# Grouped query attention with a sigmoid-routed expert layer on one core: query projections without padding, spread over partition quadrants by transfers inside SBUF

## The chip, the cores and the metric

The kernel runs on one core of one Trainium2 chip, in one launch. The metric is the device time of that core in microseconds (us). Three runs of the kernel before took 600.33, 602.37 and 600.90 us, so its median is 600.90 us. All data are float32.

Engine names: PE is TensorE (matmuls; PEld its weight loads), DVE is VectorE, ACT is ScalarE, POOL is GpSimd, SP is SyncE. SBUF and PSUM have 128 partitions each; a quadrant is 32 consecutive partitions.

## The reference, cut to what matters

`x` is (2, 1024, 256). It passes an attention layer, a layer norm, an expert layer with a shared expert, and a second layer norm:

```python
def _L0_attn_ref(x, Wq, Wk, Wv, Wo):          # 16 query heads of 16, 4 key/value heads
    q = (x @ Wq).reshape(B, T, N_HEAD, HEAD_DIM).transpose(0, 2, 1, 3)
    k = (x @ Wk).reshape(B, T, N_HEAD_KV, HEAD_DIM).transpose(0, 2, 1, 3)
    v = (x @ Wv).reshape(B, T, N_HEAD_KV, HEAD_DIM).transpose(0, 2, 1, 3)
    k = jnp.repeat(k, rep, axis=1)             # rep = 4
    v = jnp.repeat(v, rep, axis=1)
    att = jnp.einsum('bhqd,bhkd->bhqk', q, k) * scale
    att = att + alibi[None] + causal[None, None]
    att = jax.nn.softmax(att, axis=-1)
    y = jnp.einsum('bhqk,bhkd->bhqd', att, v)
    return y.transpose(0, 2, 1, 3).reshape(B, T, C) @ Wo
...
x = _layernorm(x + _L0_attn_ref(x, ...), axis=-1)
x = _layernorm(x + _L0_ffn_ref(x, ...), axis=-1)   # 8 experts, one per token, and a shared one
```

`alibi` is a slope of the head times (key position minus query position); the four query heads that share a key head have the same slope. `causal` is minus infinity above the diagonal. Only the attention layer's query projection, `x @ Wq`, and what stands around it in time are touched by the change.

## The kernel before, in words

**Tiles.** There are 16 tiles of 128 tokens, 8 for each of the two sequences `b`. A *half* `(b, i)` is four tiles, 512 tokens; there are four halves: (0,0), (0,4), (1,0), (1,4). `KC` = 2 is the number of 128-row pieces of the 256 input channels; every projection sums over both pieces `c` in PSUM.

**Layout for the scores.** A key head `g` (0 to 3) has the quadrant of partitions 32g to 32g+31. In it, partition 0 (`ROW_POS`) carries the position term, partition 1 (`ROW_MAX`) takes the negated row maximum later, and partitions 16 to 31 (`ROW_HEAD`) the 16 channels of the head. `kT` holds keys so (`wk_pad` is `Wk` with zero columns in between), and `kaug` adds the positions. `qT[b]` is 128 partitions x 4 (`r`, the query heads of a key head) x 1024 tokens. Its rows come from `wq_pad` (L128 to L137), which is `Wq` spread to 128 columns for each `r`, half of them zero. A score tile is then four matmuls side by side, one in each quadrant.

**Projections of a half.** `turn_x` (L308) transposes four token tiles on PE and copies `xT` out on ACT (L317). `do_kv` (L319) makes keys (`kpj`, two matmuls of 128x512 that DVE adds `kaug` to, L323) and values (`vpj`, eight matmuls of 128x64, copied by ACT, L334). `do_q(b, r, i)` (L336) makes two of the four `r`, each with two matmuls of 128x512 (`project`, L292 to L296), and ACT adds `qbias`, the slopes in the `ROW_POS` rows, while it copies to `qT` (L341). So a half has 8 such matmuls and 4 such activations.

**Order of the work.** PE, DVE, ACT and POOL follow an order written out by hand inside `manual_schedule` (`MANUAL`, L29); SP's is left to the scheduler in the first part and set by hand in the second. `first_projections` (L357) transposes the first half (L368, copied by ACT for c = 0 and DVE for c = 1, L369), then runs `do_kv`, both `do_q` and `turn_x` of the next half. Then `LEAD` = 10 *score units* run ahead (L843 to L853): a unit is four PSUM banks of scores (`start_s`, L388, `s_ps`), two for each pair of key heads. A unit on the diagonal has two banks masked by DVE (L427) and two copied by ACT (L435) and masked by POOL (L438), and each pair is reduced by DVE from a `diag` buffer later (L449). Any other unit is reduced by DVE straight from its four banks (L417). The ten units are those of the first half's four query tiles. Between them the projections of the other three halves are put in as *fill*: a list of pieces with costs (`projections`, L345), from which pieces are taken after unit k while `left * LEAD > total * (LEAD - 1 - k)`. All of this shares six PSUM banks (`bank`, L304), so a matmul waits until DVE or ACT has emptied the bank that it is to fill.

After the tenth unit the main loop (L854) pairs score units of later query tiles with the transposed scores `t_ps` (L485) of earlier ones. These need `join_maxima` (L456: DVE, L459), `spread_maxima` (L466: PE transposes `mT`, L470, and DVE adds `qS`, L474). Exponentials (L504, L521), the product with the values (L529), output, norm and routing follow, and the expert layer ends the kernel.

**Loads.** SP issues, in this order, the four loads of `x` (L98, L103), `Wo`, the router, the shared expert's weights (L110 to L112, three of 512 KB) and the filling of the table `slot_x` in DRAM with empty rows (L281, 3900 KB from one small tile). ACT issues `Wq`, `Wk`, `Wv` (L99 to L101) first. The shared expert's weights are first used after the score units have run out, `slot_x` when the first sequence is routed.

Of the kernel before, what the change touches and what calls it, by code (L numbers as in the profile page):

```python
# [9 lines left out]
F32 = mybir.dt.float32  # L10
I32 = mybir.dt.int32
AF = mybir.ActivationFunctionType
# [4 lines left out]
P = 128  # L17
N_HEAD = 16
N_KV = 4
REP = N_HEAD // N_KV  # L20
HD = 16
PAD = 32
ROW_POS = 0
ROW_MAX = 1
ROW_HEAD = 16
# [3 lines left out]
MANUAL = {  # L29
    mybir.EngineType.PE,  # L30
    mybir.EngineType.DVE,
    mybir.EngineType.Activation,
    mybir.EngineType.Pool,
}


# [8 lines left out]
def attn_moe_postln_kernel(  # L45
# [15 lines left out]
    nc = tc.nc  # L61
    B, T, C = x.shape
    E, _, F2 = gate_up.shape
    FF = F2 // 2
    KC = C // P
    FC = FF // P
    QT = T // P
    NTT = B * QT
# [6 lines left out]
    SLOTS = (E * OWN + NO) * P  # L75
    ROW = C + 4
    NUM, WT = C, C + 1
# [29 lines left out]

    sh_gu = const.tile([P, KC, F2], F32, tag="sh_gu", name="sh_gu")
    sh_d = const.tile([P, FC, C], F32, tag="sh_d", name="sh_d")
    nc.sync.dma_start(out=sh_gu[:, :, :FF], in_=sh_gate.rearrange("(c p) f -> p c f", p=P))  # L110
    nc.sync.dma_start(out=sh_gu[:, :, FF:], in_=sh_up.rearrange("(c p) f -> p c f", p=P))
    nc.sync.dma_start(out=sh_d, in_=sh_down.rearrange("(c p) n -> p c n", p=P))  # L112

# [9 lines left out]

    wq_pad = acon.tile([P, KC, REP, N_KV, PAD], F32, tag="wq_pad", name="wq_pad")  # L128
    wk_pad = acon.tile([P, KC, N_KV, PAD], F32, tag="wk_pad", name="wk_pad")
    nc.vector.memset(wk_pad, 0.0)  # L130
    nc.vector.memset(wq_pad, 0.0)
    for c in range(KC):
        nc.vector.tensor_scalar_mul(
            wq_pad[:, c, :, :, ROW_HEAD : ROW_HEAD + HD],
            wq_raw[:, c, :].rearrange("p (g r d) -> p r g d", g=N_KV, d=HD),
            scale,
        )  # L137
        nc.vector.tensor_copy(
            wk_pad[:, c, :, ROW_HEAD : ROW_HEAD + HD],
            wk_raw[:, c, :].rearrange("p (g d) -> p g d", d=HD),  # L140
        )
# [7 lines left out]
    for g, slope in enumerate(alibi_slopes()):  # L149
# [14 lines left out]
        out=causal,  # L164
        in_=causal,
# [97 lines left out]
    with (  # L263
# [11 lines left out]
    ):  # L275
        qT, kT, xT = {}, {}, {}

        empty = shp.tile([P, ROW], F32, tag="th", name="empty")
        nc.gpsimd.memset(empty, 0.0)
        nc.gpsimd.memset(empty[:, NUM : NUM + 1].bitcast(I32), NTT * P)  # L280
        nc.sync.dma_start(out=slot_xt, in_=empty.unsqueeze(1).broadcast_to([P, SLOTS // P, ROW]))  # L281


        def pj_tile(name):
            return ps_m.tile([P, 512], F32, tag="m", name=name)
# [1 line left out]
        def own_tiles(b, xTb):  # L287
            xT[b] = xTb
            kT[b] = qkp.tile([P, T], F32, tag="kT", name=f"kT_{b}")
            qT[b] = qkp.tile([P, REP, T], F32, tag="qT", name=f"qT_{b}")  # L290

        def project(dst, b, w, cols):  # L292
            for c in range(KC):
                nc.tensor.matmul(  # L294
                    dst, lhsT=w(c), rhs=xT[b][:, c, cols], start=(c == 0), stop=(c == KC - 1)
                )  # L296

        def wq_of(r):
            return lambda c: wq_pad[:, c, r].rearrange("p g d -> p (g d)")

        def wk_of(c):
            return wk_pad[:, c].rearrange("p g d -> p (g d)")
# [5 lines left out]
        def turn_x(b, i):  # L308
            if b not in xT:

                xTb = ptp.tile([P, KC, T], F32, tag="pT", name=f"xT_{b}")
                own_tiles(b, xTb)
            for c in range(KC):
                tp = bank("xtp")
                for j in range(4):
                    nc.tensor.transpose(tp[:, ts(j, P)], xs[:, b * QT + i + j, ts(c, P)], ident)
                nc.scalar.copy(xT[b][:, c, i * P : (i + 4) * P], tp)  # L317

        def do_kv(b, i):  # L319
            cols = slice(i * P, (i + 4) * P)  # L320
            pj = bank("kpj")
            project(pj, b, wk_of, cols)
            nc.vector.tensor_add(kT[b][:, cols], pj, kaug[:, cols])  # L323
            pv = bank("vpj")[:, : 4 * N_KV * HD].rearrange("p (j g d) -> p j g d", j=4, d=HD)
            for j in range(4):
                for c in range(KC):
                    nc.tensor.matmul(
                        pv[:, j].rearrange("p g d -> p (g d)"),
                        lhsT=xT[b][:, c, ts(i + j, P)],
                        rhs=wv_sb[:, c, :],  # L330
                        start=(c == 0),
                        stop=(c == KC - 1),
                    )
            nc.scalar.copy(vs[b][:, i : i + 4, :, 0:HD], pv)  # L334

        def do_q(b, r, i):  # L336
            cols = slice(i * P, (i + 4) * P)
            for j in range(2):
                pj = bank("qpj")
                project(pj, b, wq_of(r + j), cols)  # L340
                nc.scalar.activation(qT[b][:, r + j, cols], pj, AF.Identity, bias=qbias)  # L341

        halves = [(b, i) for b in range(B) for i in range(0, QT, 4)][1:]

        def projections():  # L345


            pieces = []
            for h, after in zip(halves, [*halves[1:], None]):
                pieces.append((11, lambda h=h: do_kv(*h)))  # L350
                pieces.append((14, lambda h=h: do_q(h[0], 0, h[1])))
                if after:
                    pieces.append((4, lambda h=after: turn_x(*h)))
                pieces.append((14, lambda h=h: do_q(h[0], 2, h[1])))
            return pieces

        def first_projections():  # L357

            own_tiles(0, xTp.tile([P, KC, T], F32, tag="xT", name="xT_0"))
            cols = slice(0, 512)  # L360
            warm = bank("warm")
            zeros = mnegs[0].rearrange("p r g d -> p (r g d)")
            for i in range(2):
                nc.tensor.matmul(warm, lhsT=zeros[:, :P], rhs=zeros, start=True, stop=True)
            for c, copy in enumerate((nc.scalar.copy, nc.vector.tensor_copy)):
                tp = bank("xtp0")
                for j in range(4):
                    nc.tensor.transpose(tp[:, ts(j, P)], xs[:, j, ts(c, P)], ident)  # L368
                copy(xT[0][:, c, cols], tp)  # L369
            do_kv(0, 0)  # L370
            do_q(0, 0, 0)
            do_q(0, 2, 0)
            turn_x(*halves[0])


# [419 lines left out]
        def gap(room):  # L795
            nonlocal slot
            after_burst()
            start_route(True)
            if products and products[0][0] <= slot:
                product(*products.pop(0)[1])  # L800
                room -= 4
            room -= 4 * maxima()
            pieces(room)
            slot += 1
# [39 lines left out]
        for k in range(LEAD):  # L844
            unit = s_queue.pop(0)
            sps = [[start_s(unit, h, j) for j in range(HALF)] for h in range(2)]
            run(*[m for hs in sps for _, m in hs])
            for h in range(2):
                end_s(unit, h, [sp for sp, _ in sps[h]], h == 1)
            while fill and left * LEAD > total * (LEAD - 1 - k):  # L850
                left -= fill[0][0]
                fill.pop(0)[1]()
            gap(0)  # L853
        for n, (b, qt, kt) in enumerate(steps):  # L854
            last = n + 1 == len(steps) or steps[n + 1][:2] != (b, qt)
            made = []
            if kt != qt:
                made.append((2 * n + 2, (b, qt, kt, kt == 0, False)))
            if last:
                ready = max(2 * n + 2, 2 * first[b, qt] + (7 if qt >= 3 else 4))  # L860
                made.append((ready, (b, qt, qt, qt == 0, True)))
            if s_queue:
                unit = s_queue.pop(0)
                for h in range(2):

                    t, s = [], []
                    for j in range(HALF):
                        t.append(start_t(b, qt, kt, h, j))
                        s.append(start_s(unit, 1 - h, j))
                    run(t[0][1], s[0][1], t[1][1], s[1][1])  # L870
                    end_t(b, qt, kt, h, [tp for tp, _ in t])
                    end_s(unit, 1 - h, [sp for sp, _ in s], h == 1)
                    if h == 1:
                        products += made
                    gap(6)
            else:

                t = [[start_t(b, qt, kt, h, j) for j in range(HALF)] for h in range(2)]
                run(*[m for hs in t for _, m in hs])
                for h in range(2):  # L880
                    end_t(b, qt, kt, h, [tp for tp, _ in t[h]])
                products += made
                wide_gap()
# [13 lines left out]
    with (  # L897
# [6 lines left out]
        tc.tile_pool(name="ps_d", bufs=2, space=PSUM) as ps_d,  # L904
        tc.tile_pool(name="ps_t", bufs=2, space=PSUM) as ps_t,
        tc.tile_pool(name="rt2", bufs=1) as rtp,
        tc.manual_schedule(engines=MANUAL | {mybir.EngineType.SP}),
    ):
        wgu = wgup.tile([P, E, KC, F2], F32, tag="wgu", name="wgu")
        wd = wgup.tile([P, E, FC, C], F32, tag="wd", name="wd")  # L910
# [386 lines left out]
```

## Time and profile before

| what | value |
|---|---|
| median of 3 runs | 600.90 us (600.33 to 602.37) |
| the profiled execution | 602.41 us, of which the span from first to last instruction is 600.7 us |
| mean granted PE clock | 0.988 of full |
| PE busy | 572.7 us, 95% of the span |
| DVE, ACT, POOL busy | 344.4, 267.0, 155.4 us |
| first matmul of a score unit | 19.74 us |
| end of the last fill piece's matmuls | 65.19 us |
| start of the second group of `mT` transposes | 69.39 us |

How to read it: the page gives busy time of each engine, then the span in 40 slices (15 us each; a digit is the busy share in tenths), the DMA queues, the chain of work that ended last, and groups of equal instructions with count, busy time, mean duration and what ended the idle time before them. An arrow `out<-in` names tiles. A matmul of 128x512 in float32 stands in the trace as two records. A record of a matmul is longer (some 600 ns) than the distance to the next (some 430 ns), since they are pipelined; the chain counts the distance.

### The profile page before, as it was taken

To read this page: it belongs to the slowest core of one execution; us is meant where nothing else is said; L and a number is where in the kernel's file an instruction comes from. 1 tells how busy PE (TensorE), PEld (TensorE's weight loads), DVE (VectorE), ACT (ScalarE), POOL (GpSimd) and SP (SyncE) were. 2 spreads that over 40 slices of the span, in tenths; PEclk is the share of its full clock that TensorE was granted. 3 is DMA by queue.
4 is the path that set the end of the run, shared out by engine and by line. 5 is a ranking of instruction groups with operands and counts; after the bars stand their busy time and mean duration, and the time that the engine had idled before them with its cause. 6 is when DMAs were issued, how large, how long until landed. Compare 5 with 4: busy or idle time off the path is not lost.

```text
span 600.7 us, 9431 instructions
## 1 busy us (share of the span) xinstructions
PE 572.7 (95%) x3708; PEld 327.8 (55%) x3708; DVE 344.4 (57%) x734; ACT 267.0 (44%) x484; POOL 155.4 (26%) x189
## 2 busy tenths in 40 slices
PE   7999999999999999999999999999999999999990
PEld 4555534444445353435356644645664788888650
DVE  3186767867776767777766845342541264444541
ACT  1433476676665656655575754554112111111120
POOL 4010222111111102013321120232111237766541
PEclk9999989999999999999999999999999999999996
DMA  9700000000000000000100000100163545752100
GB/s 311 245 1 2 2 0 2 1 1 1 2 2 1 1 1 0 3 0 28 45 1 1 3 0 1 39 33 1 35 215 98 181 160 187 242 180 79 48 19 4
DMA packets 23104, 32.66 MB, mean 54 GB/s; under 512 B 3294, under 2 KB 18948, under 8 KB 23056
## 3 DMA queue, kind: packets, MB, share of 16 engines
q1 hardware_dynamic: 18784, 25.28, 12.7%
q0 software_dynamic: 3456, 6.34, 3.0%
q8 instruction: 31, 0.51, 0.4%
q10 hardware_dynamic: 816, 0.39, 0.2%
q14 instruction: 17, 0.14, 0.1%
HBM read 22.20 MB, written 12.97 MB: 59 GB/s over the span
## 4 chain that ended last, share of the span: by engine, by line
PE 87%; DVE 7%; ACT 1%; DMA 1%; issue 1%; POOL 0%; POOLq 0%; ACTq 0%
PE t_ps L485 18%; PE yT L529 11%; PE s_ps L401 11%; PE gu_sh L688 6%; PE qpj L294 5%; PE gp L1108 5%; PE dp L1124 5%; PE up L1108 5%; PE dp_sh L708 4%; DVE past L417 3%; PE o_ps L574 2%; PE mT L470 2%; DVE past L449 1%; PE lg L599 1%; PE dp L1166 1%; PE gp L1016 1%
## 5 line engine op out<-in xcount | busy, mean ns | idle before, releaser
L401 PE MATMUL s_ps<-kT,qT 32*128 32x128 f32 (+2 forms) x1280 | 184.0, 378 | 1.2 <-DVE past L417 0.7
L417 DVE TENSOR_REDUCE past<-s_ps 128x1 f32<-128x512 f32 (+2 forms) x224 | 144.6, 686 | 61.6 <-PE s_ps L401 44.9
L485 PE MATMUL t_ps<-qS,kT 32*128 32x512 f32 x576 | 173.7, 637 | 0.6 <-ACT pD L507 0.6
L504 ACT ACTIVATE pT<-t_ps 128x512 f32<-128x512 f32 x224 | 121.6, 600 | 93.2 <-PE s_ps L401 65.0
L401 PEld LDWEIGHTS s_ps<-kT,qT 32*128 32x128 f32 x1280 | 96.2, 185 | 14.4 <-ACT pT L504 4.5
L485 PEld LDWEIGHTS t_ps<-qS,kT 32*128 32x128 f32 x576 | 53.4, 183 | 63.5 <-issue 23.7
L509 POOL TENSOR_SCALAR_AFFINE_SELECT pD<-pD 128x1024 f32<-128x1024 f32 x32 | 34.8, 1093 | 101.8 <-ACT pD L507 101.6
L529 PE MATMUL yT<-pT,v 128*32 128x512 f32 x448 | 59.7, 605 | 0.0
L438 POOL TENSOR_SCALAR_AFFINE_SELECT diag<-diag 128x1024 f32<-128x1024 f32 x16 | 17.5, 1094 | 134.8 <-ACT diag L435 114.1
L233 POOL TENSOR_TENSOR rstd<-rstd,neg_half 128x1 f32<-128x1 f32 x36 | 20.6, 571 | 115.1 <-DVE rstd L232 113.3
L507 ACT COPY pD<-t_ps 128x512 f32<-128x512 f32 x64 | 34.7, 600 | 24.5 <-PE s_ps L401 13.9
L688 PE MATMUL gu_sh<-x1T,sh_gu 128*128 128x512 f32 x96 | 43.5, 596 | 0.0
L239 POOL DMA_INDIRECT slot_x<-xs,slots x32 | 32.1, 1004 | 42.0 <-DVE slots L669 24.3
L449 DVE TENSOR_REDUCE past<-diag 128x8 f32<-128x1024 f32 x32 | 38.6, 1211 | 0.0
L521 ACT ACTIVATE pD<-pD 128x1024 f32<-128x1024 f32 x32 | 33.9, 1067 | 0.2 <-POOL pD L509 0.2
L1116 ACT ACTIVATE sg<-gp 128x512 f32<-128x512 f32 x16 | 9.6, 597 | 54.6 <-PE gp L1108 54.6
L1108 PE MATMUL gp<-slot_xT,wgu 128*128 128x256 f32 x128 | 30.4, 381 | 1.2 <-ACT slot_xT L1077 1.2
L1108 PE MATMUL up<-slot_xT,wgu 128*128 128x256 f32 x128 | 30.2, 379 | 0.0
L294 PE MATMUL qpj<-xT,wq_pad 128*128 128x512 f32 x64 | 29.1, 601 | 0.1
L1124 PE MATMUL dp<-wd,slot_h 128*128 128x256 f32 x128 | 29.0, 379 | 0.0
L427 DVE TENSOR_TENSOR diag<-s_ps,causal 128x512 f32<-128x512 f32 x32 | 20.6, 685 | 13.9 <-PE s_ps L401 13.9
L1053 POOL DMA_INDIRECT zt<-z_dram,row x20 | 20.8, 1041 | 27.8 <-issue 27.8
(170 smaller groups left out, 665.7 us busy)
## 6 DMA issues: line engine op xcount, KB each, us to landing
wgu<-_L_ffn_gate_up_proj_dram SPq DMA_DIRECT2D x8, 1024.0 KB, 9.8
wd<-in_L_ffn_down_proj_dram SPq DMA_DIRECT2D x8, 512.0 KB, 5.8
slot_x<-empty SPq DMA_DIRECT2D x1, 3900.0 KB
row<-slot_x SPq DMA_DIRECT2D x8, 260.0 KB, 2.9
xs<-in_L_attn_x_dram SPq DMA_DIRECT2D x4, 512.0 KB, 7.8
z_dram<-z_sh SPq DMA_DIRECT2D x12, 128.0 KB, 1.8
row<-slot_x SPq DMA_DIRECT2D x4, 130.0 KB, 2.0
sh_gu<-L_ffn_shared_gate_w_dram SPq DMA_DIRECT2D x1, 512.0 KB
```

The lines of the kernel that those rows point to most:

```text
L294: nc.tensor.matmul(dst, lhsT=w(c), rhs=xT[b][:, c, cols], start=(c == 0), stop=(c == KC - 1))
L401: lambda r=r: nc.tensor.matmul(sp[:, r * n * P : (r + 1) * n * P], lhsT=qT[b][rows, r0 + r, ts(qt, P)], rhs=kT[b][rows, key * P : (key + n ...
L417: nc.vector.tensor_reduce(past[:, h * HALF + j, r0 : r0 + nr, parts[b, qt][key]], sp[j].rearrange("p (r k) -> p r k", r=nr), AX.X, ALU.max ...
L449: lambda: nc.vector.tensor_reduce(past[:, gs, :, 0], diag[:, gs], AX.X, ALU.max, negate=True),
L485: lambda: nc.tensor.matmul(tp, lhsT=kT[b][rows, ts(kt, P)], rhs=qS[b, qt][rows].rearrange("p r q -> p (r q)"), start=True, stop=True,)
L504: nc.scalar.activation(p[:, j], tp[j], AF.Exp)
L507: nc.scalar.copy(p[:, j], tp[j])
L509: nc.gpsimd.affine_select(out=p, in_=p, pattern=[[0, HALF * REP], [1, P]], compare_op=ALU.is_ge, fill=MASKED, base=0, channel_multiplier=-1,)
L529: nc.tensor.matmul(yTs[b, qt][g * PAD : (g + 1) * PAD], lhsT=vs[b][:, kt, g, :], rhs=p[:, g, :], start=start, stop=stop,)
L688: nc.tensor.matmul(gu[k], lhsT=sh_gu[:, c, col : col + P], rhs=x1T[:, c, ts(tb, TB)], start=(c == 0), stop=(c == KC - 1),)
L1108: nc.tensor.matmul(dst[:, j], lhsT=wgu[:, e, c, col : col + P], rhs=xT[:, c, :], start=(c == 0), stop=(c == KC - 1),)
L1124: nc.tensor.matmul(dp, lhsT=h[:, f, ts(i, P)], rhs=wd[:, e, f, :], start=(f == 0), stop=(f == FC - 1),)
```

## The change

The 16 query heads are projected without padding: `wq_r` has 256 columns per c, ordered (r, g, d). One matmul has 128 full columns, that is two values of `r`, so a half takes 4 matmuls of 128x512 (m = 0, 1; c = 0, 1). The result stands with 16 rows for each (r, g), not in quadrants. ACT copies it to a staging tile `q_all` in a buffer of the `pT` tag (for m = 1 of the first half DVE does), and eight DMAs of 64 KB each (16 partitions x 2 x 512) take it from there to the `ROW_HEAD` rows of `qT`. Of the first half, four are issued by SP and four by ACT; of the other halves, all by SP. All rows of `qT` are written before that with `qbias` (`other_rows`): by ACT for the first half, after its first `xT` copy, and by POOL for the other three.

`first_projections` runs `do_q` ahead of `do_kv`. SP's order is now written out by hand in the first part too. The three loads of the shared expert, the two POOL memsets of `empty` and the filling of `slot_x` come after the ten score units. The fill pieces are now (14, kv), (14, q) and (4, turn) for a half in place of (11, kv), (14, q), (4, turn), (14, q).

```diff
@@ MANUAL
+    mybir.EngineType.SP,
@@ loads
-    nc.sync.dma_start(out=sh_gu[:, :, :FF], in_=sh_gate.rearrange("(c p) f -> p c f", p=P))
-    nc.sync.dma_start(out=sh_gu[:, :, FF:], in_=sh_up.rearrange("(c p) f -> p c f", p=P))
-    nc.sync.dma_start(out=sh_d, in_=sh_down.rearrange("(c p) n -> p c n", p=P))
@@ weights
-    wq_pad = acon.tile([P, KC, REP, N_KV, PAD], F32, tag="wq_pad", name="wq_pad")
+    wq_r = acon.tile([P, KC, REP, N_KV, HD], F32, tag="wq_r", name="wq_r")
...
-    nc.vector.memset(wq_pad, 0.0)
     for c in range(KC):
         nc.vector.tensor_scalar_mul(
-            wq_pad[:, c, :, :, ROW_HEAD : ROW_HEAD + HD],
+            wq_r[:, c],
...
@@ start of the attention part
-        empty = shp.tile([P, ROW], F32, tag="th", name="empty")
-        nc.gpsimd.memset(empty, 0.0)
-        nc.gpsimd.memset(empty[:, NUM : NUM + 1].bitcast(I32), NTT * P)
-        nc.sync.dma_start(out=slot_xt, in_=empty.unsqueeze(1).broadcast_to([P, SLOTS // P, ROW]))
...
+        def other_rows(b, i, copy):
+            copy(qT[b][:, :, i : i + 512], qbias.unsqueeze(2).broadcast_to([P, REP, 512]))
...
-        def wq_of(r):
-            return lambda c: wq_pad[:, c, r].rearrange("p g d -> p (g d)")
+        def wq_of(m):
+            return lambda c: wq_r[:, c, 2 * m : 2 * m + 2].rearrange("p r g d -> p (r g d)")
@@ turn_x, when b = 1 begins
                 own_tiles(b, xTb)
+                for j in range(0, T, 512):
+                    other_rows(b, j, nc.gpsimd.tensor_copy)
@@ do_q
-        def do_q(b, r, i):
+        def do_q(b, i):
             cols = slice(i * P, (i + 4) * P)
-            for j in range(2):
+            stage = ptp.tile([P, N_KV, 512], F32, tag="pT", name="q_all")[:, :2]
+            for m in range(2):
                 pj = bank("qpj")
-                project(pj, b, wq_of(r + j), cols)
-                nc.scalar.activation(qT[b][:, r + j, cols], pj, AF.Identity, bias=qbias)
+                project(pj, b, wq_of(m), cols)
+                if (b, i) == (0, 0) and m == 1:
+                    nc.vector.tensor_copy(stage[:, m], pj)
+                else:
+                    nc.scalar.copy(stage[:, m], pj)
+            to = qT[b].rearrange("p (m r) t -> p r m t", r=2)
+            for r in range(2):
+                for g in range(N_KV):
+                    row = (r * N_KV + g) * HD
+                    queue = nc.scalar if (b, i, r) == (0, 0, 1) else nc.sync
+                    queue.dma_start(
+                        out=to[g * PAD + ROW_HEAD : g * PAD + ROW_HEAD + HD, r, :, cols],
+                        in_=stage[row : row + HD],
+                    )
@@ projections
-                pieces.append((11, lambda h=h: do_kv(*h)))
-                pieces.append((14, lambda h=h: do_q(h[0], 0, h[1])))
+                pieces.append((14, lambda h=h: do_kv(*h)))
+                pieces.append((14, lambda h=h: do_q(*h)))
                 if after:
                     pieces.append((4, lambda h=after: turn_x(*h)))
-                pieces.append((14, lambda h=h: do_q(h[0], 2, h[1])))
@@ first_projections
+            other_rows(0, 0, nc.scalar.copy)
+            other_rows(0, 512, nc.gpsimd.tensor_copy)
+            do_q(0, 0)
             do_kv(0, 0)
-            do_q(0, 0, 0)
-            do_q(0, 2, 0)
             turn_x(*halves[0])
@@ after the ten score units
+        nc.sync.dma_start(out=sh_gu[:, :, :FF], in_=sh_gate.rearrange("(c p) f -> p c f", p=P))
+        nc.sync.dma_start(out=sh_gu[:, :, FF:], in_=sh_up.rearrange("(c p) f -> p c f", p=P))
+        nc.sync.dma_start(out=sh_d, in_=sh_down.rearrange("(c p) n -> p c n", p=P))
+
+        empty = shp.tile([P, ROW], F32, tag="th", name="empty")
+        nc.gpsimd.memset(empty, 0.0)
+        nc.gpsimd.memset(empty[:, NUM : NUM + 1].bitcast(I32), NTT * P)
+        nc.sync.dma_start(out=slot_xt, in_=empty.unsqueeze(1).broadcast_to([P, SLOTS // P, ROW]))
```

More of the change, by code (lines that the diff above doesn't have):

```diff
@@ L906, in attn_moe_postln_kernel @@
         tc.tile_pool(name="rt2", bufs=1) as rtp,
-        tc.manual_schedule(engines=MANUAL | {mybir.EngineType.SP}),
+        tc.manual_schedule(engines=MANUAL),
     ):
```

## The prediction

> **What bounds the kernel now.** I read the page's busy shares and slices first.
>
> ```profile
> PE 572.7 (95%) x3708; PEld 327.8 (55%) x3708; DVE 344.4 (57%) x734; ACT 267.0 (44%) x484; POOL 155.4 (26%) x189
> ...
> PE   7999999999999999999999999999999999999990
> ...
> DVE  3186767867776767777766845342541264444541
> ...
> PEclk9999989999999999999999999999999999999996
> DMA  9700000000000000000100000100163545752100
> ```
>
> PE is full in all slices but the first and last, so matmul time taken out shortens the run unless another engine takes over where it was. The transfers are concentrated in the first two slices; the queues are empty from 28 us on. Next, the groups of the first 71 us.
>
> ```profile
> L294 PE MATMUL qpj<-xT,wq_pad 128*128 128x512 f32 x64 | 29.1, 601 | 0.1
> L341 ACT ACTIVATE qT<-qpj,qbias 128x512 f32<-128x512 f32 x16 | 11.0, 687 | 22.1 <-PE qpj L294 22.1
> L449 DVE TENSOR_REDUCE past<-diag 128x8 f32<-128x1024 f32 x8 | 9.6, 1212 | 0.0
> L435 ACT COPY diag<-s_ps 128x512 f32<-128x512 f32 x8 | 4.3, 588 | 2.0 <-PE s_ps L401 2.0
> ```
>
> The query projections are 64 records. Their price is the distance between records, which the chain of waits of 0 to 110 us gives:
>
> ```profile
> 7.71 0.72 DVE kaug L158
> 8.43 0.07 DVE qbias L153
> 8.49 0.61 DVE xT L369
> 9.10 0.04 issue
> 9.15 1.12 PE kpj L294 x2
> 10.27 1.73 PE vpj L327 x16
> 12.00 6.92 PE qpj L294 x16
> 18.92 0.87 PE xtp L316 x8
> ```
>
> 6.92 / 16 = 0.4325 us a record. PE starts at 9.15 us on the DVE copy of `xT`, and from there to the first score matmul at 19.95 us it is PE alone. From there on the chain is nearly PE alone to 66.77 us; there it goes to DVE for 2.6 us (last reductions, `mneg`) before the second group of `mT` transposes at 69.39 us.
>
> [...]here the 128 KB `z_dram` stores issued by SP took 1.8 us, the 130 KB `row` loads 2.0 us[...]. [...]here an issue takes some 0.44 us on SP, 0.55 on ACT. [...]the windows show 0.50 at 78 to 80 us, after a stretch of short PE waits.
>
> **The change, part by part.**
>
> *Matmuls.* Half of the 64 records go: 8 of each half's 16, 8 x 0.4325 = 3.46 us a half, 13.8 us in all.
>
> *The start, to the first score matmul.* DVE loses the 0.91 us memset of `wq_pad`, worth nothing: it then waited for `Wq` (2.9 us) and `Wk` (1.1 us). The `xT` copy still ends at 9.10 us. `qpj` c = 0 runs before that, as `kpj` c = 0 did. From 9.15 PE has 6 records of q (to some 11.9), 4 of keys, values and transposes: 8 records fewer, so scores could start at 19.95 - 3.46 = 16.5 us. Now the transfers. ACT's `qbias` fill waits for `qbias` (8.5 us) and writes 2048 columns: from the 1.07 us of 1024 columns (L521) about 2.0, to 10.6; its copy of m = 0 follows to 11.3, hidden under PE's m = 1. DVE copies m = 1 from 11.95 to 12.65. Both queues start at 12.7; the fourth issue starts at 12.7 + 3 x 0.44 = 14.0 (SP) and 12.7 + 3 x 0.55 = 14.4 (ACT); with 2.0 us to landing, 16.4. The cover is `do_kv` and the transposes, which end at 16.5, so the transfers cost nothing, with no spare; each us later is a us lost. Behind ACT's four issues stands only the value copy, needed after 15.4. The older loads are no obstacle: [...]these 2.7 MB are in by about 10 us at the 251 to 394 GB/s that the windows show. Gain: **3.4 us**.
>
> *The lead (ten score units with fill).* PE loses 3 x 3.46 = 10.4 us. But DVE keeps its work, and the new piece list bunches it. With costs 92 in all, the rule of the fill leaves nothing after units 2, 4 and 7, so units 2 and 3, 4 and 5, 7 and 8 stand back to back; before, a piece followed every unit but unit 1 and the last (units are counted from 0). Two units ask DVE for up to eight reductions of 0.62 us within 2.2 us of PE time, and six banks do not hold that. I walked the engines' orders with these durations (unit 1.08 us of PE; L417 0.62, L449 1.13, L427 0.63, ACT copy 0.54), each matmul starting when its bank, or its `xT`, is free. PE then stands still: 1.06 us before unit 3 (banks of unit 2), 2.36 us before the keys of half (1,0), 0.66 in unit 5, 0.51 in unit 6, 0.81 before the keys of (1,4), 0.66 in unit 8, 0.18 in unit 9, and 1.16 + 0.27 before the first `t_ps` (DVE is late with `qS`), then 0.35 + 0.87 to the second `mT`: 8.9 us. The 2.36 has this chain: unit 3's diagonal goes to a `diag` buffer that DVE frees only after four reductions of unit 2 (2.5 us) and one L449; ACT's copies wait for it, the `xT` copies stand behind them on ACT, and the key matmul behind those. The same walk of the kernel before gives 2.5 us of waits (0.52, 0.41, 0.31, 0.35, 0.87) and the second `mT` at 67.8, where the trace has 69.39; I use only the difference. Gain: 10.4 - (8.9 - 2.5) = **4.0 us**.
>
> *Copies.* ACT loses 16 activations of 0.69 and gets 7 copies of 0.6 and DVE one: ACT waits for PE in this stretch (22.1 us of idle time before L341), worth nothing. *POOL's fills* of 2048 columns: bound from 2.1 us (its 1024-column L438 takes 1.09)[...]; they stand ahead of the first and the fourth mask of the lead, more than 5 and 10 us before these are due; nothing[...]. *Later halves' transfers*: eight issues by SP, about 3.5 us, plus 2.0; the earliest user, the first query tile of half (0,4), comes 30 us later. *New waits*: three first users of `pT` buffers on ACT and one `qS` on DVE now wait for eight DMA semaphores that are long set[...]; value: in the range. *Loads put off*: they are issued behind the last queries' transfers, some 59 us, and run some 20 us next to work that uses no transfers; first use is beyond 250 us, and the same fill at 8 to 28 us showed no waits. Between 0 and 2 us[...]; I take 0. After the second `mT` the orders of PE, DVE, ACT and POOL are unchanged, so the shift stays.
>
> Sum: 3.4 + 4.0, unrounded 7.3 us. The profiled execution took 602.41 (span 600.7, 1.7 around it), hence 595.1; the median shown is 1.5 below that execution: 600.9 - 7.3 = **593.6 us**.
>
> **The rivals.**
> *All of PE's time comes back.* 3.4 + 10.4 = 13.8: 587.1 us. For it: DVE's total in the lead is only about 32 us (24 x 0.62 + 8 x 1.13 + 8 x 0.63 and small ones) of the 44 left. Against: the waits are from bunching, not from the sum.
> *Transfers late, or the clock.* If landing takes 6 us, scores start at 18.8, and the walk leaves 3.8 us: 597.1; issues of 1.2 us each leave 5.6. A drop to half clock for 3 us after the waits near 27 to 32 us costs up to 1.5. For it: no transfer from SBUF to SBUF is in the trace, the schedule has no spare. Against: 64 KB is half of the smallest transfer seen.
> *Slower: transfers of a queue run one after the other.* If each lands before the next moves, the fourth lands at 12.7 + 4L; the gain is gone at L = (16.5 + 7.3 - 12.7) / 4 = 2.8 us. At 3.5 us the first scores start at 26.7, 10.2 late: 603.8 us. Against: the `x` loads of one queue overlapped.
> *It does nothing*: the matmuls are counted out by the program, so only collisions of the put-off loads could eat it: 600.9.
>
> **Chances.** Forecast 0.66; all of it 0.10; late or clock 0.18; nothing 0.03; slower 0.03. 0.3% of 600.9 is 1.8 us, about what a measurement of this kernel can tell from no change: faster means under 599.1. The first three lie there: 0.94; same 0.03, slower 0.03. Range: the walk's lengths are good to perhaps 2 us; downward 3.2 us towards the first rival (half of its distance), upward to the late case, 597.1: 590.4 to 597.1.
>
> **What would show it.** `qpj` with 32 records; first score matmul at 16.5 (later, with idle time ended by a DMA: the late case); a PE wait of about 2.4 us before `kpj` near 30 us, ended by ACT, and short ones ended by DVE in units 3, 5, 6, 8; second `mT` some 7.3 us earlier and the same distance at the end. Wrong if the lead shows few waits (first rival), if the clock falls in it, or if the shift changes after the second `mT`.

## The result, and the profile after

| | before | after |
|---|---|---|
| median of 20 runs each, side by side | 600.96 us (599.92 to 603.85) | 598.18 us (594.97 to 602.31) |
| ratio, 95% interval | | 0.9958 (0.9942 to 0.9974) |
| the profiled execution (its span) | 602.41 (600.7) | 598.39 (596.7) |
| mean granted PE clock in it | 0.988 | 0.985 |
| second group of `mT` transposes | 69.39 us | 67.36 us |
| from there to the end of the span | 531.3 us | 529.3 us |

The kernel became faster by 2.8 us, where 7.3 were forecast. The first page lines say that the matmuls did go, and where PE lost something else (compare the same rows of before, in the prediction):

```profile
PE 563.7 (94%) x3676; PEld 326.0 (55%) x3676; DVE 342.6 (57%) x734; ACT 261.7 (44%) x476; POOL 161.1 (27%) x192
...
PE   7989999999999999999999999999999999999990
...
DVE  2266877777776758687767844342551264444541
...
PEclk9799999999999999999999999999999999999996
DMA  6122490000000000001100000100062536652100
```

PE has 32 records fewer and is busy 9.0 us less, but the span is only 4.0 us shorter: the other 5.0 us are idle time that was not there before. In PE's second slice (15 to 30 us) the digit is still 9, but the granted clock is 0.7; its third slice (30 to 45 us) is no longer full (8). The DMA row shows the loads put off in the slices from 60 us on. The groups of the first 71 us:

```profile
L291 PE MATMUL qpj<-xT,wq_r 128*128 128x512 f32 x32 | 15.1, 608 | 1.4 <-DVE xT L382 1.2 <-ACT xT L382 0.2
...
L287 POOL COPY qT<-qbias 128x2048 f32<-128x2048 f32 x3 | 5.6, 1890 | 2.6 <-DVE qbias L151 2.6
...
L346 ACT COPY q_all<-qpj 128x512 f32<-128x512 f32 x7 | 4.1, 586 | 14.4 <-PE qpj L291 14.4
```

32 query records, as forecast; POOL's fills take 1.89 us each. The chain of waits shows what happened in the second slice:

```profile
12.19 0.70 DVE q_all L344
...
12.96 0.74 SPq L352
...
13.75 0.83 SPq L352
...
14.62 4.15 DMA qT<-q_all
...
18.82 2.77 PE s_ps L415 x28
21.59 3.71 PE kpj L291 x4
25.30 1.99 PE vpj L326 x16
27.29 1.10 PE s_ps L415 x32
...
67.36 0.66 PE mT L484 x4
```

The columns are start, length, what. The last line is the second group of `mT` transposes; the chain of before has it later:

```profile
69.39 0.66 PE mT L470 x4
```

Up to 12.89 us all is within 0.3 us of the forecast (12.65). Then SP issues in steps of about 0.8 us, where 0.44 was taken, and the transfer on the chain takes 4.15 us from issue to landing, where 2.0 was taken. PE comes to the first score at 16.81 us (16.5 was forecast), but after two matmuls it waits for one transfer after the other, and the scores run together only from 18.82. Then a second thing: the four key records take 3.71 us, and those of half (1,0), further down this chain, 1.99. The windows (PE, PEld, DVE, ACT, POOL busy; granted PE clock; DMA share; GB/s) say why:

```profile
16.00:18.00 2.00, 1.51 (x11) 1.03 (x9) 0.17 (x1) 1.15 (x3) 0.00 (x0) 1.00 0.88 110
18.00:20.00 2.00, 1.30 (x12) 0.94 (x14) 0.00 (x0) 0.00 (x0) 0.00 (x0) 0.72 0.00 0
20.00:22.00 2.00, 2.00 (x27) 1.78 (x24) 0.69 (x2) 0.68 (x2) 0.00 (x0) 0.50 0.03 8
...
24.00:26.00 2.00, 2.00 (x8) 1.24 (x7) 0.66 (x1) 0.00 (x0) 0.00 (x0) 0.57 0.00 0
```

PE waits for the transfers between 16 and 19 us, and then works at half clock from 18.9 to 25.7. Last, PE's waits from 18 to 68 us (in all, times, longest):

```profile
PE kpj L291 <- ACT xT L316: 2.5, 2, 1.8
PE s_ps L415 <- DVE past L431: 1.2, 3, 0.6
PE s_ps L415 <- DMA qT<-q_all: 1.1, 2, 0.7
PE t_ps L499 <- DVE qS L488: 0.3, 1, 0.3
```

The waits before the keys of the other sequence's halves, ended by ACT, and those for DVE are there, but shorter than the walk of the prediction had them: the longest is 1.8 us instead of 2.36, and the units wait three times for DVE, 1.2 us in all, where it had five waits with 3.1. The third line is the forecast's gap: transfers were to cost nothing.

After's 20 runs lie in three groups, by their mean clock: one at 0.990 (594.97 us), thirteen at 0.985 to 0.988 (596.6 to 599.16), six at 0.980 to 0.981 (600.35 to 602.31). A stretch at half clock lasts 3.4 us in the trace of before (from 77 us on), with 1.7 us lost, and 6.8 us in that of after, at a price of 2.8 us (experiment 1). From these numbers I estimate that a good part of the spread is the number of such stretches.

### The profile page after: what moved, and what is told of

Same layout as the page of the kernel before. It is cut to its first block, busy times and chain, and to the rows that moved or that the text cites. A ratio compares the mean times of both kernels' runs of the same rounds, so it can differ in the third digit from the quotient of the medians.

```text
span 596.7 us, 9436 instructions
## 1 busy us (share of the span) xinstructions
PE 563.7 (94%) x3676; PEld 326.0 (55%) x3676; DVE 342.6 (57%) x734; ACT 261.7 (44%) x476; POOL 161.1 (27%) x192
## 4 chain that ended last, share of the span: by engine, by line
PE 84%; DVE 9%; ACT 2%; DMA 2%; issue 1%; POOL 0%; SPq 0%; POOLq 0%; ACTq 0%; DVEq 0%
PE t_ps L499 18%; PE s_ps L415 11%; PE yT L543 11%; PE gu_sh L702 6%; PE gp L1132 5%; PE dp L1148 5%; PE up L1132 5%; DVE past L431 4%; PE dp_sh L722 4%; PE o_ps L588 2%; PE qpj L291 2%; DVE past L463 2%; PE mT L484 1%; PE kpj L291 1%; PE lg L613 1%; PE dp L1190 1%
## 5 line engine op out<-in xcount | busy, mean ns | idle before, releaser
L415 PE MATMUL s_ps<-kT,qT 32*128 32x128 f32 (+2 forms) x1280 | 188.7, 382 | 3.2 <-DVE past L431 1.9
L415 PEld LDWEIGHTS s_ps<-kT,qT 32*128 32x128 f32 x1280 | 99.4, 188 | 16.6 <-DVE past L431 5.7
L452 POOL TENSOR_SCALAR_AFFINE_SELECT diag<-diag 128x1024 f32<-128x1024 f32 x16 | 17.5, 1093 | 125.2 <-ACT diag L449 104.5
L702 PEld LDWEIGHTS gu_sh<-x1T,sh_gu 128*128 128x128 f32 x96 | 17.4, 190 | 18.1 <-issue 18.1
```

The source lines that it names most:

```text
L415: lambda r=r: nc.tensor.matmul(sp[:, r * n * P : (r + 1) * n * P], lhsT=qT[b][rows, r0 + r, ts(qt, P)], rhs=kT[b][rows, key * P : (key + n ...
L702: nc.tensor.matmul(gu[k], lhsT=sh_gu[:, c, col : col + P], rhs=x1T[:, c, ts(tb, TB)], start=(c == 0), stop=(c == KC - 1),)
```

## The experiments

The theory after the result: the transfers end 3.3 us later than the forecast needed, and the waits that this makes let the clock fall, which costs about as much again; the lead came out as forecast. Rivals: the lead's waits alone ate the gain; the loads put off collide later; or the clock has nothing to do with the waits. Each ratio below is to the kernel before, run beside it on the same chip. That kernel has a median of 602.85 us beside experiments 1 to 4, 600.59 beside 5 to 8 and 601.99 beside 9 to 11, so runs of different groups are compared by their ratios; the changed kernel's is 0.9958. Line numbers in a profile are those of the kernel shown.

**1. PE kept busy while the transfers run** (`hold` is a PSUM tile that nobody reads).

```diff
         nc.vector.tensor_copy(rwT, rps)
+        hold = ps_y.tile([P, 512], F32, tag="y", name="hold")
+        zeros = mnegs[0].rearrange("p r g d -> p (r g d)")
+        for i in range(2):
+            nc.tensor.matmul(hold, lhsT=zeros[:, :P], rhs=zeros, start=True, stop=True)
         fill = projections()
```

> The changed kernel with two matmuls of 128x512 on zeros put between the router's transposes and the first score unit; they compute nothing that is used. My theory: the first scores wait some 1.9 us for the transfers, and that wait makes the granted PE clock fall to half for some 6.8 us, which costs 3.4 us more. Then the two matmuls (1.73 us) fill the wait, the first unit still ends its wait near 18.8 us, but the clock between 18 and 26 us stays at 1.00, the first unit ends near 19.9 instead of 21.6, and the time is 598.2 - 3.4 = about 594.8 us. Rival (the fall of the clock has nothing to do with this wait, or the loss lies in the lead where DVE holds PE up): clock 0.5 as before, about 598 us or up to 1.7 more.

Measured: 598.17 us, ratio 0.9938 (0.9909 to 0.9968), by ratio some 1 us under the changed kernel, where 3.4 were expected. The total is a miss, and the windows, with a line of the chain, show the theory half right:

```profile
18.00:22.00 4.00, 3.73 (x37) 2.18 (x36) 1.23 (x2) 1.08 (x2) 0.08 (x1) 1.00 0.04 5
22.00:26.00 4.00, 4.00 (x51) 3.22 (x50) 1.14 (x3) 0.68 (x2) 1.02 (x1) 1.00 0.00 0
34.00:38.00 4.00, 2.34 (x3) 1.18 (x4) 2.28 (x3) 2.05 (x4) 2.81 (x2) 0.71 0.36 56
38.00:42.00 4.00, 4.00 (x36) 3.05 (x36) 1.82 (x2) 0.37 (x1) 1.95 (x2) 0.87 0.00 0
...
24.49 1.10 PE s_ps L415 x32
```

With PE busy up to the first scores the clock stays whole there (1.00), and unit 1 starts at 24.49 us instead of 27.29: 2.8 us earlier, the price of the fall. But in this execution the clock falls at the next wait instead, before the keys of half (1,0) (0.71), and the second `mT` is only 1.1 us earlier than in the changed kernel. The changed kernel has the same wait, of 1.8 us, and keeps its clock there:

```profile
36.00:38.00 2.00, 0.67 (x7) 0.43 (x4) 2.00 (x3) 1.15 (x3) 0.01 (x1) 1.00 0.66 110
```

So a filled wait does not rule out a fall at another one, and a wait does not always bring a fall.

**2. No wait at all: the next half's keys and values put ahead of the first scores.**

```diff
             for h, after in zip(halves, [*halves[1:], None]):
-                pieces.append((14, lambda h=h: do_kv(*h)))
+                if h != halves[0]:
+                    pieces.append((14, lambda h=h: do_kv(*h)))
...
             turn_x(*halves[0])
+            do_kv(*halves[0])
```

> The changed kernel with the keys and values of the second half taken out of the fill and put ahead of the first score unit, so that PE has 3.6 us of real work while the transfers travel. My theory: first scores at about 20.6 us with no wait for a transfer, clock at 1.00, so both the wait (1.9) and the clock's price (3.4) are gone: 598.2 - 5.3 = about 592.9 us; the pieces left also fall more evenly between the units, which could give another 1 us. Rival (the loss is the bunching in the lead): only the evener pieces help, about 597 us.

Measured: 590.87 us, ratio 0.9806 (0.9782 to 0.9829).

```profile
18.82 1.73 PE vpj L326 x16
20.55 0.15 PE rps L855
20.71 1.06 PE s_ps L417 x29
```

The work added there (3.7 us) ends at 20.55; scores start at 20.71 without a wait for a transfer, no stretch at half clock remains before the tail of the program (the granted clock is 1.00 up to 577.5 us), and the second `mT` stands at 58.90, 8.5 us earlier than in the changed kernel. Of these, 5.5 are won at the start (the theory had 5.3): unit 0 ends at 21.77 with the next keys and values done, and the changed kernel gets there at 27.29. The other 3.0 come from the lead, which is left with a piece less to bunch: PE's waits from 16 to 58 us are 1.5 us in all, against 5.1 from 18 to 68. The runs' clocks agree: in the three kernels without a wait for the first transfers (experiments 2, 6 and 11) 10 of 15 runs have a mean clock of 0.990 or more, in the changed kernel (with experiment 8) 3 of 30.

**3. All eight first transfers issued by SP.**

```diff
-                    queue = nc.scalar if (b, i, r) == (0, 0, 1) else nc.sync
+                    queue = nc.sync
```

> The changed kernel with all eight transfers of the first half issued by SP. An issue took 0.6 us, so the last starts 4 x 0.6 = 2.4 us later, and the first unit ends its wait at about 21.2 us. My theory: the transfers stand on the path, so this costs up to 2.4 us; the fall of the clock is there already and does not get dearer: about 600.5 us. Rival (the transfers are covered by other work or only their landing counts): 598.2 us.

Measured: 600.89 us, ratio 0.9972 (0.9940 to 1.0004), by ratio 0.8 us above the changed kernel and not to be told from it; that the median is near the 600.5 expected is due to this chip, where before is slower too. The end of the chain to the first scores:

```profile
16.98 0.60 SPq L352
...
17.62 2.41 DMA qT<-q_all
...
20.07 0.93 PE s_ps L415 x18
```

The first of these lines is the seventh issue, the second the eighth with its landing. Alone, SP needs 0.64 us from issue to issue (16.98 to 17.62), and a transfer 2.41 us. The last lands at 20.02; with two queues, in executions at full clock, it lands at 19.35 (experiment 5) and 19.59 (experiment 1). The second queue puts four of the eight issues, some 2.4 us, beside the others, and saves 0.4 to 0.7 us (0.6 counted from the first issue), not the 2.4 of the theory. The windows of the changed kernel and of this one show a reason:

```profile
15.00:17.50 2.50, 2.15 (x18) 1.73 (x17) 0.17 (x1) 1.45 (x3) 0.00 (x0) 1.00 1.02 159
15.00:17.50 2.50, 2.29 (x22) 1.95 (x22) 0.17 (x1) 1.45 (x3) 0.00 (x0) 1.00 0.66 104
```

With two queues the DMA engines' share is 1.02, so the view shows no idle time of theirs (under the loads of before it goes up to 1.11, from 20 to 24 us); with one it is 0.66. This does not explain all: from 18 us on the engines of the changed kernel carry nothing (0.00 in its window 18 to 20), and its last landings come at 18.77 us and later.

**4. First half padded as before, the others by transfers.**

```diff
-            other_rows(0, 0, nc.scalar.copy)
             other_rows(0, 512, nc.gpsimd.tensor_copy)
-            do_q(0, 0)
             do_kv(0, 0)
+            for r in range(REP):
+                pj = bank("qpj")
+                project(pj, 0, lambda c: wq_pad[:, c, r].rearrange("p g d -> p (g d)"), cols)
+                nc.scalar.activation(qT[0][:, r, cols], pj, AF.Identity, bias=qbias)
             turn_x(*halves[0])
```

(`wq_pad` is kept beside `wq_r` for it.)

> The changed kernel with the first half alone projected as before: padded weights beside the dense ones, eight matmuls, bias by ACT, keys and values ahead of the queries, no transfers for that half; the other three halves as in the changed kernel. My theory: first scores at 20.0 us as in the kernel before, clock 1.00, and the lead gives its 4.0 us: 600.9 - 4.0 = about 596.9 us. Rival (DVE holds PE up in the lead more than worked out): 599 to 601 us.

Measured: 597.68 us, ratio 0.9924 (0.9900 to 0.9949).

```profile
21.18 1.06 PE s_ps L424 x29
...
65.94 0.66 PE mT L493 x4
```

This is the lead alone. From the end of unit 0 (22.23 us) to the second `mT` (65.94) it takes 43.7 us; the kernel before takes 48.4 (21.01 to 69.39). Gain 4.7 us, where 4.0 was forecast: the lead is not where the forecast failed. (Unit 0 ends later than in before because this execution ran at half clock from 7.7 to 11.1 us: 0.52 on average from 7.5 to 11.) The start, with its transfers and its clock, brings nothing that these runs can tell: ratio 0.9924 without it, 0.9958 with it.

**5. Finer fill pieces** (keys 8, values 7, and 7 for each m of the queries).

```diff
-                pieces.append((14, lambda h=h: do_kv(*h)))
-                pieces.append((14, lambda h=h: do_q(*h)))
+                pieces.append((8, lambda h=h: do_k(*h)))
+                pieces.append((7, lambda h=h: do_v(*h)))
+                pieces.append((7, lambda h=h: do_q(*h, [0])))
+                pieces.append((7, lambda h=h: do_q(*h, [1])))
```

(`do_kv` is split into `do_k` and `do_v` for it, and `do_q` takes the list of its m.)

> The changed kernel with its fill cut finer: keys (8), values (7), each half of the queries (7, 7) and the transposes (4) are pieces of their own, so that nearly every score unit of the lead is followed by a piece; the start is not touched. My theory: the waits of PE on DVE and ACT in the lead (8.9 us in my walk) shrink by about 4 us, the wait for the first transfers and its clock stay: about 4 us under the changed kernel beside it. Rival (the waits in the lead are DVE's sum, not its bunching, or the loss lies only at the start): within 1 us of the changed kernel.

Measured: 593.11 us, ratio 0.9859 (0.9835 to 0.9883); 5.0 us below the changed kernel beside it. PE's waits from 18 to 68 us:

```profile
PE kpj L291 <- DVE diag L455: 1.4, 1, 1.4
PE s_ps L429 <- DMA qT<-q_all: 1.0, 2, 0.7
PE kpj L291 <- ACT xT L316: 0.7, 1, 0.7
```

The waits for DVE in the units are gone and the sum, with one of 0.3 us not shown, falls from 5.1 to 3.4 us; the wait for the transfers stays. But the fall of the clock does not stay with it (two windows, then two lines of the chain):

```profile
17.50:20.00 2.50, 1.48 (x20) 1.13 (x24) 0.00 (x0) 0.00 (x0) 0.00 (x0) 1.00 0.06 5
20.00:22.50 2.50, 2.50 (x24) 1.42 (x20) 1.29 (x2) 1.08 (x2) 0.82 (x1) 1.00 0.02 7
...
24.25 1.10 PE s_ps L429 x32
...
61.00 0.59 PE mT L498 x4
```

The edit does not touch this place, and the expectation was that the fall would stay. The second `mT` is 6.4 us earlier than in the changed kernel: 3.0 by the start of unit 1 (24.25 instead of 27.29), mostly from the clock, and 3.3 in the lead. The runs fit this: at a clock of 0.990 they are 3.5 us under those of experiment 8, and more of them are at 0.987 and above (5 of 5, against 3 of 10). A good part of the lead's waits was thus made by bunching, not by DVE's sum of work.

**6. Experiments 2 and 5 together.** Its edit is the two diffs above.

> Both together: keys and values of the second half ahead of the first score unit, and the fill cut finer. My theory: no wait for transfers, clock at 1.00 there, and the evener lead worth another 1 us over the kernel with the keys and values ahead, whose ratio to the kernel before was 0.981: ratio about 0.979, some 590 us. Rival (finer pieces cost more than they give): 0.981 or above.

Measured: 587.93 us, ratio 0.9779 (0.9756 to 0.9801). The fastest kernel of the study; its waits from 16 to 58 us are 0.5 us in all, with the same work for DVE. So the lead's waits come from the order of the pieces.

**7. The loads and the filling of `slot_x` issued early again**, ahead of the first transfers.

```diff
+        nc.sync.dma_start(out=sh_gu[:, :, :FF], in_=sh_gate.rearrange("(c p) f -> p c f", p=P))
...
+        nc.sync.dma_start(out=slot_xt, in_=empty.unsqueeze(1).broadcast_to([P, SLOTS // P, ROW]))
...
-        nc.sync.dma_start(out=sh_gu[:, :, :FF], in_=sh_gate.rearrange("(c p) f -> p c f", p=P))
...
-        nc.sync.dma_start(out=slot_xt, in_=empty.unsqueeze(1).broadcast_to([P, SLOTS // P, ROW]))
```

> The changed kernel with the loads of the shared expert and the filling of the table issued by SP where the kernel before has them, ahead of the first half's transfers. My theory: four of the eight transfers then stand behind 5.4 MB in the same queues, which took until 27 us in the kernel before; first scores at about 28 us, some 9 us later than in the changed kernel, with the clock at half after it: about 608 us. Rival (the transfers interleave with the loads, so putting the loads off was not needed): within 2 us of the changed kernel.

Measured: 608.76 us, ratio 1.0122 (1.0093 to 1.0152), 10.7 us above the changed kernel beside it. The chain:

```profile
9.10 18.47 DMA slot_x<-empty
...
27.59 2.30 DMA qT<-q_all
...
30.02 2.04 PE s_ps L424 x26
```

On the chain, the last query transfer is issued at 27.59 us, when the whole filling has landed (27.57): that is what putting the loads off avoids. In the kernel before the filling ran at the same time and PE had no wait of over 0.6 us from 19 to 70 us: no query passed through a DMA.

**8. Control: the changed kernel once more**, beside 5, 6 and 7.

> The changed kernel itself, as a measure on the same chip as the others: ratio 0.996 to the kernel before. In its runs the time should fall as the mean granted clock rises[...].

Measured: 598.11 us, ratio 0.9948 (0.9921 to 0.9975). Its ten runs are sorted by clock again: 0.990 gives 594.97 and 595.12; 0.985 gives 598.1 to 598.7; 0.980 and 0.981 give 600.67 and 602.33. The kernel before on the same chip has 600.6 us on average in its four runs at 0.990. At 0.990 the change is thus worth 5.6 us, though by two of its runs only; at 0.985 and 0.986 it is worth 4.7 (five runs with 598.3 on average, against 602.9 in before's four at 0.986). In the medians it is worth 2.5, since it runs more often at a lower clock. Its trace repeats that of the changed kernel: the same waits, and half clock from 19.1 us for 6.8 us.

**9. Only the finer fill, in the kernel before** (padded queries, no transfers).

```diff
-                pieces.append((11, lambda h=h: do_kv(*h)))
-                pieces.append((14, lambda h=h: do_q(h[0], 0, h[1])))
-                if after:
-                    pieces.append((4, lambda h=after: turn_x(*h)))
-                pieces.append((14, lambda h=h: do_q(h[0], 2, h[1])))
+                pieces.append((8, lambda h=h: do_k(*h)))
+                pieces.append((7, lambda h=h: do_v(*h)))
+                for r in range(REP):
+                    pieces.append((7, lambda h=h, r=r: do_q(h[0], r, h[1], 1)))
+                    if r == 1 and after:
+                        pieces.append((4, lambda h=after: turn_x(*h)))
```

(`do_kv` is split as in experiment 5, and `do_q` gets the number of its r.)

> The kernel before, with its padded projections and nothing else changed but the fill cut finer (keys 8, values 7, each r of the queries 7, transposes 4). My theory: its lead has only some 2.5 us of waits, since PE has 10.4 us more to do there, so the finer fill gives at most 1 us: ratio 0.998 to 1.000. Rival (the finer fill is worth what it gave the changed kernel, 5 us, whatever the projections): ratio about 0.992.

Measured: 598.65 us, ratio 0.9955 (0.9940 to 0.9969), between the two expectations and so a miss for both. PE has no wait in its lead, the second `mT` stands at 67.21, 2.2 us earlier, and most of its 19 runs (13) have a clock of 0.990 or more, against 9 of 24 of before beside it. A new list of pieces in the old kernel brings as much as the whole change (0.9955 and 0.9958).

**10. ACT's four first transfers left out** (one run). The kernel leaves out the queries of two of each four heads for the first 512 tokens.

```diff
+                    if (b, i, r) == (0, 0, 1):
+                        continue
-                    queue = nc.scalar if (b, i, r) == (0, 0, 1) else nc.sync
+                    queue = nc.sync
```

> The changed kernel without the four transfers of the first half that ACT issues: the queries of two of each four heads are missing for the first 512 tokens of the first sequence, so its output is not the reference's. It measures the transfers alone. If two queues at once slow each other (issues 0.74 to 0.83 us apart in place of 0.6, landing 3.6 us in place of 2.3), SP's four now start 0.6 us apart and land by about 12.96 + 3 x 0.6 + 2.4 = 17.2 us, next to no wait being left. If each transfer is slow by itself at that place, the last lands near 19 us as before.

Measured: 596.33 us in its one run. The chain:

```profile
13.65 0.59 SPq L354
...
14.92 2.29 DMA qT<-q_all
...
17.35 1.12 PE s_ps L417 x26
```

Without a second queue beside it, SP's second issue takes 0.59 us instead of 0.83 and the last transfer lands 2.29 us after its issue instead of 4.15. The DMA engines' share from 15 to 17.5 us is 0.45, against 1.02. So the eight transfers at once slow each other, and one of this size is not slow by itself. Whether it is the two queues or the bytes, of which half are missing too, this run does not separate. Even so the scores that are left run together 0.85 us later than the forecast's 16.5.

**11. Experiment 6 with one queue.** Edit: that of experiment 3.

> Keys and values of the second half ahead, finer fill, and all eight first transfers issued by SP. With one queue the last transfer landed at about 20.1 us, and the first scores of this version start at 20.4 us behind the keys and values. My theory: the second queue is then not needed: the same ratio as with two queues, 0.978. Rival (one queue costs the 2.4 us of four more issues): about 0.982.

Measured: 589.17 us, ratio 0.9796 (0.9769 to 0.9823), against 0.9779 (0.9756 to 0.9801): the intervals overlap, and the times don't tell the two apart. In the traces the second `mT` stands at 57.25 us with one queue and at 57.33 with two.

## Why the prediction was wrong, point by point

In the profiled executions the forecast of 7.3 us became 4.0 (spans), and the pieces can be read off the traces:

| term | us |
|---|---|
| forecast | 7.3 |
| transfers late, and what goes with them: unit 0 would have ended at 16.5 + 1.05 = 17.55; at full clock (experiment 1) it ends at 20.85 | -3.3 |
| half clock at the first scores: unit 1 at 27.29 instead of 24.49 (experiment 1) | -2.8 |
| lead better than the walk: 4.7 instead of 4.0 (experiment 4) | +0.7 |
| after the second `mT`: 531.3 before, 529.3 after; before's own fall of the clock at 77 to 81 us (1.7 us lost) isn't in this execution | +2.0 |
| sum | 3.9 |

Experiment 5, whose clock stayed whole at the start too, gives 3.1 and 3.0 for the second and third line. Before's own fall, in its windows (from 74 to 77 us PE was busy for 2.38 of 3 us):

```profile
78.00:80.00 2.00, 2.00 (x10) 0.34 (x7) 0.67 (x1) 2.00 (x4) 0.18 (x1) 0.50 0.00 0
```

That it fell in the one execution that was profiled and not in the other is luck; without it the +2.0 would be 0.3.

- **Wrong: the transfers.** The failed step is the start: "the transfers cost nothing, with no spare". SP's last transfer was to land at 16.0 us and landed at 19.35 (experiment 5): 2.1 us from the landing (4.1 instead of 2.0), 1.0 from the issues (0.74, 0.83 and 0.61 with both engines issuing instead of 0.44, which came from loads of another kind), 0.2 from a later start. So the term that was mis-sized most is the landing, and experiment 10 has it at 2.29 again with half of the transfers. The cover, keys and transposes up to 16.5 us, was sized rightly. The argument that 64 KB is half of the smallest transfer seen was a misreading: before's page has loads of 64 KB (`Wk`, `Wv`) and 8 KB. The second queue saved 0.4 to 0.7 us (experiment 3). The time of the issues is not small beside that of a transfer: eight small transfers took SP alone 4.6 us up to the start of the eighth issue, and one transfer 2.4.
- **Wrong: the clock.** It stood only in a rival, near 27 to 32 us, at up to 1.5 us. It fell at 18.9 us, right after the waits for the transfers, for 6.8 us, and cost 2.8; a fall in the lead was one of the forecast's own signs of being wrong. Just before the fall, from 15.4 to 18.8 us, PE was busy for 2.24 of 3.40 us, and no single wait was longer than 0.69. Fewer waits go with fewer falls in experiment 2 and in the runs' clocks (0.990 or more in 10 of 15 runs without the first wait, in 3 of 30 with it). But the same waits had no fall in experiment 5, and the changed kernel's longest wait had none, while PE was busy for only 0.67 of the 2 us from 36 to 38. So the share of idle time alone does not decide it; what does is open.
- **The rival "Transfers late, or the clock"** named both causes. With scores at 18.8 us it left 3.8 us of gain; it had the two as alternatives, and in the traces of the changed kernel and of experiment 8 they come together.
- **Right: the matmuls.** 32 records went. (The sum has a slip without weight: 3.46 and 3.95 make 7.4, not 7.3.)
- **Right: the lead**, to 0.7 us, with its longest wait (1.8 us, 36.67 to 38.46) before the keys of half (1,0) and ended by ACT's `xT`. The rival that all of PE's time comes back is refuted by the same waits; experiment 5 shows that it needs another list of pieces.
- **Right: POOL's fills** (1.89 us each, lower than the 2.1 taken), **the copies, the later halves' transfers** (landing in 2.3 us in the median and 3.6 at most, no wait for them) **and the loads put off.** From 70 to 80 us the DMA engines are busy for 0.97 of the time; the distance from the second `mT` to the end did not grow.
- **Refuted: a queue's transfers one after the other.** On one queue the eighth issue began 4.6 us after the first and landed 2.41 later; at one by one with 2.3 us each they would have taken 18. Of the four `x` loads, the prediction's argument, the traces show that they were on their way together (in the changed kernel issued from 0.8 to 2.4 us, each landing 4.8 to 7.8 us after its issue), not whether they moved at the same time.

The spread of the runs sets a bound to this reading: the table holds for one pair of executions. In the medians the gain is 2.8 us, because the changed kernel runs more often at a low clock: beside experiment 8, before has 10 of 15 runs at 0.989 or more, the changed kernel 2 of 10. At the same clock it is 4.7 to 5.6 (experiment 8), near 7.3 - 3.3 + 0.7 = 4.7.

## What to carry to other kernels

When a matmul chain is replaced by a shorter one and a transfer, sum the issues too, with durations taken while the other queue issues (SP's second took 0.83 us so, and 0.59 alone), and leave a spare of some us of PE work before the first user: 3.7 us of work moved there was worth more than the change itself (experiment 2). Where PE is the bound, price each new wait once for its length and once more, as a chance, for a stretch at half clock after it (2.8 us here), and look at the other waits too when one is filled. A list of pieces that is spread between units should be spread finely before anything is taken out of it (experiments 5 and 9).

## What the runs showed of the hardware that was not expected

- Small transfers from SBUF to SBUF (64 KB, 16 partitions) land 2.3 to 2.4 us after their issue in most cases on one queue (a median of 2.3 over SP's 28 in the changed kernel, 2.41 for the last of experiment 3), and in 3.2 to 4.2 us when SP and ACT issue four each at the same time; the DMA engines' share from 15 to 17.5 us is then 1.02, against 0.66 with one queue. An issue on SP takes 0.59 us, 0.74 when it is the first of the group, and 0.83 for the second beside ACT's.
- Waits of PE that are each at most 0.72 us were followed by 6.8 us at half clock in two traces (the changed kernel and experiment 8) and by none in a third (experiment 5). One kernel's runs, with the same program, then differ by up to 7.3 us (594.97 at a mean clock of 0.990, 602.31 at 0.981), the time falling as the mean clock rises.
